# A gated recurrence dissolved into the end of the convolution and into the masked attention of a decoder kernel

## The chip, the cores and the metric

One core of a Trainium2 chip runs the whole program. The metric is the device time of one execution in microseconds. Before the change three runs took 3234.93, 3235.93 and 3240.06 us; their median, 3235.93 us, is the time before. About 0.2% (6.5 us) is what such a measurement can tell from no change.

## The reference, cut to what matters

The model is a decoder of four layers with three sublayers each, on x of 128 sequences x 64 tokens x 128 features, all in float32. Every sublayer ends as `x = layernorm(x + f(x))`. The change concerns three neighbours: the convolution with experts that ends layer 2 (`L2_ffn`), the gated recurrence that begins layer 3 (`L3_attn`), and the masked cross-attention after it (`L3_xattn`). The recurrence is

```python
xn = x / jnp.maximum(jnp.sqrt(jnp.sum(x * x, -1, keepdims=True)), 1e-12) * jnp.sqrt(128.) * gamma
q, kv, a = jnp.split(jnp.einsum('bnd,ed->bne', xn, W_qkva), 3, axis=-1)
# h[n] = sigmoid(a[n]) * h[n-1] + kv[n], along the 64 tokens of a sequence
out = q * h
```

The masked attention has 16 heads of 8 features over 64 keys, with a boolean mask of its own for each sequence, an output projection and a bias. The convolution sublayer has a router, eight small experts (SiLU), an RMS norm and a small GELU bottleneck.

## The kernel before, in words

The 8192 tokens are cut into 16 chunks (`NC`) of 512 tokens, that is 8 sequences; `X[c]` holds chunk c in SBUF, token on the partition, throughout. Sublayers follow one another as functions in a list `steps`; each loops over the chunks in a software pipeline that is written out by hand. Each engine takes its instructions in one order. This order follows the program text, except that a scheduler may move an instruction forward to fill a hole that it foresees; `tc.issue_after(i)` keeps what is inside behind instruction i if it runs on the same engine.

PSUM is used in two rings: `wide` tiles (pool psA, five banks) for scores and expert outputs, and `bank` tiles (pool psB, three banks) for everything else. A `bank` tile is the one that was given out three requests ago, so the matmul that fills it waits until that earlier tile has been read. SBUF work tiles come by tag from `SPACES` in the same way (most tags have two buffers, `r` has three).

**The convolution, `ffn_conv` (from L1620).** Eight turns of two chunks. A turn i computes eight groups of expert outputs (`units`, L1687: two matmuls of 512 columns and two bias matmuls on TensorE, two SiLU on ScalarE, one product of 1024 columns on VectorE, sums on VectorE and GpSimd) and takes in between the steps of two generators: `begin(i + 1)`, the convolution and routing of the next turn, and `end(i - 1)`, the end of the turn before. `end` has these steps: two transposes of the expert sums; two output projections `z`, with square and row sum; the RMS root together with the layernorm root of the turn before that (`norm`, L1757: one Newton chain on VectorE for both); then for each chunk the scaling of `acc` by the root and `normw` (L1735, four VectorE instructions of 128 columns), the transposes of `acc` on TensorE and the new residual on GpSimd; the down projection with GELU; the up projection and the residual sum (L1753). The main loop deals them out by `take` at the groups g of the next turn: two at g = 1, three at g = 3, two at g = 6, one at g = 7, the rest at g = 0 of the turn after. The end of the last turn runs alone after the loop (L1800).

**The recurrence, `attn_scan` (from L1808).** A stage of its own, 20 turns. A turn i does in this order: row sum of the squares of chunk i and layernorm statistics of chunk i - 4 (VectorE); the squares of chunk i + 1 (ScalarE, L1839); one Newton chain for both roots (`rsqrt`, L335, eleven small VectorE instructions); the scaling of chunk i by its root (two blocks on ScalarE, L1864, two on GpSimd, L1866); the normalised chunk i - 4 written back to X (ScalarE, L378); `recalled(i - 3)`, which transposes h back on TensorE and adds X (L1835); `project(i - 1)`: four transposes, the multiplication by gamma (ScalarE, L330), q, kv and gate as three matmuls of 512 columns (L1816, L1819), the sigmoid (ScalarE, L1821), a zero at every sequence start (GpSimd, L1823), the recurrence itself as one VectorE scan instruction over 512 columns (L1825) and its product with q (L1826).

**The masked attention, `xattn_masked` (from L1499), in the frame `mha` (from L1118).** The loop runs c from -2 to 16 and works on three chunks at once. TensorE's order in one iteration: second part of the weights of chunk c's first half, transposes of chunk c + 2 (`load`), `values(c - 1, 1)` (L1268), scores of the first half of chunk c + 1 (L1193) with their mask matmuls (L1529), transposes of the attention output of chunk c - 1, values of v (L1170), `weights(c, 1)` (L1231, mask L1535, maxima L1243), `values(c, 0)`, scores of the second half of chunk c + 1, projections q and k of chunk c + 2 (L945), the output projection (L1331), the first weights of chunk c + 1 up to the point where they need the maxima `mT` (L1218, copied by VectorE, L1220). VectorE reduces each group of scores to maxima (L1201), unpacks the masks (L1517), divides (L1273, L1282) and does the layernorm; ScalarE does the exponentials (L1250) and copies; four places `aside(c, k, ...)`, k = 0 to 3, let foreign work in. Before the change that is `kept` alone: the routing of the last sublayer, from c = 2 on one step at k = 2, from c = 11 on many.

Of the kernel before, what the change touches and what calls it, by code (L numbers as in the profile page):

```python
# [234 lines left out]
def tile_decoder(ctx: ExitStack, tc: tile.TileContext, a, out):  # L235
# [882 lines left out]
    def mha(prepare, wv, finish, mask=None, diff=False, aside=lambda c, k, seen: None):  # L1118
# [166 lines left out]
        on, late, spread = range(NC), (), None  # L1285
        for c in range(-2, NC + 1):
# [17 lines left out]
            if c in on:  # L1304
                weights(c, 1)
                behind = values(c, 0)
            aside(c, 2, (behind, spread))
# [191 lines left out]
    def xattn_masked():  # L1499
# [7 lines left out]

        def prepare(c, s):
            m = work("t1", (P, BPC * 2 * S // 4), "mu").bitcast(U8), VX[c % 2][:, used + 512 : used + 768].bitcast(U8)
            for x, src in zip(m, rows_of):  # L1510
                for g in range(4):
                    nc.sync.dma_start(out=x[32 * g : 32 * g + 32], in_=src[c])
            then = begin(c, s)

            def step(n):
                f = (work("ye", (P, 512), "mf") if n == 0 else VX[c % 2][:, used : used + 512]).bitcast(BF16)
                V.tensor_scalar(f, m[n], 0.0, NEG, ALU.is_equal, ALU.mult)  # L1517
                store[c, n] = f.rearrange("p (b n k) -> p b n k", b=BPC, n=2)
                return then(n)

            return step

        def mask(c, hf, s, t):
# [16 lines left out]
            mask=mask, aside=kept,  # L1540
# [79 lines left out]
    def ffn_conv():  # L1620
# [83 lines left out]
        def end(i):  # L1704
# [27 lines left out]
            for n in pair:  # L1732
                h = acc[n]
                for t in range(TPC):
                    V.scalar_tensor_tensor(h[:, t, :], h[:, t, :], y[:, 0, n, t : t + 1], row("normw"), ALU.mult, ALU.mult)  # L1735
                hT.append(transposed(h, "oT"))
                b = with_bias(2 * i + n, "upb")
                G.tensor_tensor(b, b, h, ALU.add)
                base.append(b)
                yield  # L1740
# [35 lines left out]
        for i in range(turns):  # L1776
            b = begin(i + 1) if i + 1 < turns else none
            e = end(i - 1) if i else none
            for g in range(8):
# [10 lines left out]
                elif g == 4:  # L1790
                    take(b, 2)
                elif g == 5:
                    take(b)
                elif g == 6:
                    take(e, 2)
                elif g == 7:
                    take(e)
            tail = e
        take(tail)
        for _ in end(turns - 1):  # L1800
            pass
# [6 lines left out]
    def attn_scan():  # L1808
        w = W[9]
        xs, hs, rs = {}, {}, {}  # L1810
        kept = work("h", (P, 8, 512), "scan")

        def project(c):
            xT = transposed(xs.pop(c), "xT", scale=col("gamma"))
            q = bank("q_ps")
            mm(q, w[:, 0, :], xT, start=True, stop=True)  # L1816
            ps = [wide("kva_ps") for _ in range(2)]
            for k in range(2):
                mm(ps[1 - k], w[:, 2 - k, :], xT, start=True, stop=True)  # L1819
            g = work("qT", name="gate")  # L1820
            A.activation(g, ps[1], AF.Sigmoid)  # L1821

            G.memset(g.rearrange("p (b s) -> p b s", b=BPC)[:, :, 0:1], 0.0)  # L1823
            h = hs[c] = kept[:, c % 8]
            V.tensor_tensor_scan(h, g, ps[0], 0.0, ALU.mult, ALU.add)  # L1825
            V.tensor_tensor(h, h, q, ALU.mult)  # L1826

        def recalled(c):
            h = hs.pop(c)
# [4 lines left out]
            r = rs[c] = work("r", (P, TPC, D))  # L1834
            V.tensor_tensor(r, y.rearrange("p (t d) -> p t d", t=TPC), X[c], ALU.add)  # L1835

        def squares(c):
            s = xs[c] = work("tmp", (P, TPC, D), "sq")
            A.activation(s, X[c], AF.Square)  # L1839


        squares(0)
        for i in range(NC + 4):
            v = sm.tile([P, 2, TPC], F32, tag="lnv2", name="lnv2")
            a_, b_ = i, i - 4
            if a_ < NC:
                V.tensor_reduce(v[:, 0], xs[a_], AX.X, ALU.add)
                V.tensor_scalar(v[:, 0], v[:, 0], 1e-24, None, ALU.max)
            else:
                G.memset(v[:, 0], 1.0)  # L1850
            if b_ >= 0:
                r = rs.pop(b_)
                mv = ln_stats(r, v[:, 1])
            else:
                G.memset(v[:, 1], 1.0)
            if a_ + 1 < NC:
                squares(a_ + 1)
            y = rsqrt(v.rearrange("p n t -> p (n t)"), 2 * TPC, "rms")
            if a_ < NC:
                V.tensor_scalar(y[:, :TPC], y[:, :TPC], math.sqrt(D), None, ALU.mult)  # L1860
                xn = xs[a_] = work("o", (P, TPC, D), "xn")
                for t in range(TPC):
                    if t % 2:
                        A.activation(xn[:, t, :], X[a_][:, t, :], AF.Identity, scale=y[:, t : t + 1])  # L1864
                    else:
                        G.tensor_scalar(xn[:, t, :], X[a_][:, t, :], y[:, t : t + 1], None, ALU.mult)  # L1866
            if b_ >= 0:
                ln_apply(b_, r, mv, y[:, TPC:], on_act=True)
            if 0 <= i - 3 < NC:
                recalled(i - 3)  # L1870
            if 0 <= i - 1 < NC:
                project(i - 1)
# [28 lines left out]
    def ffn_switch():  # L1901
# [8 lines left out]
        attn_alibi, xattn_padded, ffn_conv, attn_scan, xattn_masked, ffn_switch,  # L1910
# [25 lines left out]
```

## Time and profile before

| | us |
|---|---|
| median of three runs | 3235.93 |
| profiled execution | 3240.21 |
| its span | 3238.4 |
| recurrence alone on the engines, from 2542.0 to 2650.0 of the span | 108.0 |
| `mT` of chunk 0 and of chunk 11 copied (L1220) | 2673.74 and 2877.68 |

The profile comes from one hardware-traced execution. Times within it are microseconds from the start of the span. A row of a group names the line, the engine (PE is TensorE, PEld its weight loads, DVE VectorE, ACT ScalarE, POOL GpSimd, SP the queue that issues most DMAs), the operation, output <- input, shapes and count; then the busy time, the mean of one in ns, and the idle time of that engine just before with what ended it. A timeline row is start, duration, instruction, and in brackets the idle time before it. A row of a table of stretches gives for each engine the busy time and, in brackets, the number of instructions, then the granted TensorE clock (1 is full speed) and DMA. Matmul durations overlap: the pitch from one start to the next is what a matmul costs. The copies of `mT` mark the masked attention: one per iteration, the first at the end of iteration c = -1.

### The profile page before, as it was taken

The numbers are of one execution on the slowest core, as the hardware profiler recorded it, in microseconds if no ns is written. First come the engines' busy times: TensorE is split into PE (matmuls) and PEld (weight loads), VectorE is DVE, ScalarE is ACT, GpSimd is POOL, SyncE is SP. The second block draws the span as 40 slices with busy tenths as digits, with TensorE's granted clock in tenths as the row PEclk, the third lists the DMA queues.
The fourth block names the chain that finished last, engine by engine and source line by source line (L and its number), as shares of the span: only waits on it lengthen the run. The fifth ranks groups of instructions, "written<-read, shape, count | busy, mean of one in ns | idle before, by whom it ended". The sixth has DMA issues, their size and how long they took to land. (4 is left out here: it accounts for less than half of the span.)

```text
span 3238.4 us, 110324 instructions
## 1 busy us (share of the span) xinstructions
PE 2889.3 (89%) x47200; PEld 2120.7 (65%) x47200; DVE 1979.3 (61%) x7116; ACT 1638.5 (51%) x3130; POOL 1470.8 (45%) x1500
## 2 busy tenths in 40 slices
PE   5999899988887999999999989998888669997993
PEld 3789866656666777666677767763444337776893
DVE  3732289767776666332366656666778876675245
ACT  3444388745444555333356545643445546654453
POOL 4477554245554444211244445556666223336154
PEclk9999999999998999999999989988998789998997
DMA  5578711000003000000000000000000000001584
GB/s 143 153 210 261 224 52 34 8 2 3 3 3 93 4 4 4 4 1 1 14 4 4 4 5 4 4 12 1 1 1 7 4 1 19 18 13 59 182 263 143
DMA packets 142459, 159.23 MB, mean 49 GB/s; under 512 B 16720, under 2 KB 118096, under 8 KB 141968
## 3 DMA queue, kind: packets, MB, share of 16 engines
q1 hardware_dynamic: 128064, 123.65, 12.8%
q0 software_dynamic: 13184, 27.03, 3.3%
q8 instruction: 370, 6.06, 0.8%
q10 hardware_dynamic: 720, 1.50, 0.2%
q14 instruction: 121, 0.99, 0.1%
HBM read 121.44 MB, written 30.67 MB: 47 GB/s over the span
## 5 line engine op out<-in xcount | busy, mean ns | idle before, releaser
L1201 DVE TENSOR_REDUCE m<-s_ps 128x8 f32<-128x512 f32 x640 | 397.5, 684 | 146.3 <-PE s_ps L1529 50.5
L1250 ACT ACTIVATE e<-t_ps 128x512 f32<-128x512 f32 x640 | 329.9, 601 | 152.9 <-PE t_ps L1243 152.4
L1268 PE MATMUL av_ps<-vx,e 128*64 128x18 f32 (+1 forms) x10240 | 341.1, 216 | 7.3 <-issue 7.3
L1268 PEld LDWEIGHTS av_ps<-vx,e 128*64 128x64 f32 x10240 | 322.5, 140 | 28.1 <-issue 21.5
L1145 POOL TENSOR_SCALAR eb<-qT,small 128x512 f32<-128x512 f32 x80 | 131.5, 1643 | 432.6 <-ACT qT L948 197.6
L774 ACT ACTIVATE hT<-h_ps,aux 128x256 f32<-128x256 f32 x496 | 207.1, 470 | 219.6 <-PE h_ps L772 124.6
L1231 PE MATMUL t_ps<-eb,kT 32*64 32x128 f32 x10240 | 283.4, 287 | 6.6 <-ACT e L1250 2.2
L805 POOL DMA_INDIRECT got<-l_rout,pli x192 | 193.0, 1005 | 178.0 <-issue 64.4
L380 POOL TENSOR_SCALAR x<-xb,lnmv,ln_y 128x128 f32<-128x128 f32 x240 | 188.7, 798 | 173.6 <-DVE ln_y L345 173.6
L772 PE MATMUL h_ps<-ebT,rw 128*128 128x256 f32 x992 | 243.5, 390 | 14.4 <-DVE ebT L760 10.0
L1231 PEld LDWEIGHTS t_ps<-eb,kT 32*64 32x64 f32 x10240 | 200.2, 133 | 72.9 <-DVE m L1201 25.2
L785 PEld LDWEIGHTS yg<-rw,hT 128*128 128x128 f32 x1984 | 241.5, 192 | 6.4
L785 PE MATMUL yg<-rw,hT 128*128 128x128 f32 x1984 | 241.9, 275 | 0.0
L1193 PE MATMUL s_ps<-eb,qT 32*64 32x256 f32 x5120 | 217.4, 399 | 18.2 <-POOL eb L1145 9.6
L380 POOL TENSOR_SCALAR x<-r,lnmv,ln_y 128x128 f32<-128x128 f32 x100 | 79.4, 807 | 293.3 <-DVE ln_y L345 246.9
L786 DVE TENSOR_TENSOR yo<-yg,aux 128x256 f32<-128x256 f32 x124 | 52.5, 424 | 260.8 <-PE yg L785 260.7
L1273 DVE RECIPROCAL rc<-av_ps 128x32 f32<-128x32 f32 (+1 forms) x192 | 61.7, 322 | 244.5 <-PE av_ps L1268 244.1
L772 PEld LDWEIGHTS h_ps<-ebT,rw 128*128 128x128 f32 x992 | 184.1, 196 | 38.3 <-DVE ebT L760 12.6
L747 POOL DMA_INDIRECT aux<-in_x_dram,plt x156 | 158.3, 1015 | 60.4 <-issue 26.1
L1143 ACT ACTIVATE eb<-qT,small 128x512 f32<-128x512 f32 x160 | 106.8, 715 | 128.9 <-POOL qT L1370 123.6
L1145 POOL TENSOR_SCALAR eb<-kT,small 128x512 f32<-128x512 f32 x80 | 145.3, 1816 | 21.8 <-ACT kT L950 10.9
L1193 PEld LDWEIGHTS s_ps<-eb,qT 32*64 32x64 f32 x5120 | 114.4, 134 | 57.1 <-POOL eb L1145 13.4
(437 smaller groups left out, 6446.1 us busy)
## 6 DMA issues: line engine op xcount, KB each, us to landing
rw<-in_l0w_dram SPq DMA_DIRECT2D x78, 512.0 KB
rw<-in_l3w_dram SPq DMA_DIRECT2D x46, 512.0 KB
l_rout<-yo SPq DMA_DIRECT2D x124, 128.0 KB
aux<-xd SPq DMA_DIRECT2D x46, 128.0 KB
aux<-in_l0b_dram SPq DMA_DIRECT2D x78, 66.0 KB
xd<-vx SPq DMA_DIRECT2D x5, 1024.0 KB
x<-in_x_dram SPq DMA_DIRECT2D x16, 256.0 KB
cin<-in_ctx_dram SPq DMA_DIRECT2D x16, 256.0 KB
```

Source lines behind the costliest of these rows:

```text
L380: (V if on_dve else G).tensor_scalar(X[c][:, t, :], r[:, t, :], mv[:, t, 0:1], y[:, t : t + 1], ALU.subtract, ALU.mult)
L747: s.gather = G.indirect_dma_start(out=eb[:, i, :], out_offset=None, in_=x[:, :], in_offset=bass.IndirectOffsetOnAxis(ap=tokens[:, 2 * g + ...
L772: s.pe = mm(ps[:, j * GR : (j + 1) * GR], w1[:, (k + j) * P : (k + j + 1) * P], ebT, start=True, stop=True)
L774: s.act_ins = A.activation(hT[k + j], ps[:, j * GR : (j + 1) * GR], s.act, bias=v[:, k + j : k + j + 1])
L785: s.pe = mm(y[:, i * P : (i + 1) * P], hT[k][:, i * P : (i + 1) * P], w2[:, k, :], start=(k == 0), stop=(k == FK - 1))
L805: s.gather = G.indirect_dma_start(out=got[i][k][:, t, :], out_offset=None, in_=s.rout[b][:, :], in_offset=bass.IndirectOffsetOnAxis(ap=whe ...
L1145: ins = (G if h == 2 else V).tensor_scalar(dst, x, mine, None, ALU.mult)
L1193: mm(ps[g][j * S : (j + 1) * S, u * 256 : (u + 1) * 256].rearrange("p (h k) -> p h k", h=4), rows32(s["q"], g)[:, b], rows32(s["eb"], g)[: ...
L1201: last = V.tensor_reduce(s["m"][:, g, 2 * hf : 2 * hf + 2, :].rearrange("p t h -> p (t h)"), ps[g].rearrange("p (n k) -> p n k", k=S), AX. ...
L1231: mm(ps[g][i * S : (i + 1) * S].rearrange("p (a u j q) -> p a u j q", u=2, a=2, j=2)[:, :, u, j, :], rows32(s["k"], g)[:, b], rows32(s["eb ...
L1250: last = A.activation(e[:, g, :], ps[g], AF.Exp, scale=scale)
L1268: mm(av[j * S : (j + 1) * S, 8 * (u - u0) + n, :], ev[:, n // 2, n % 2, u, j, :], vx[:, 2 * (2 * hf + u) + j, n, :], start=True, stop=True,)
```

## The change

The function `attn_scan` and its place in `steps` go. A class `Scan` has five steps for a chunk, and a call runs those that have not been run: `root` (squares, row sum, layernorm statistics of chunk c - 2, one Newton chain for both), `scale` (the scaling by the root, and chunk c - 2 normalised into X), `turn` (transposes, gamma), `run` (three matmuls, sigmoid, scan, product) and `sum` (h transposed and added to X in place). The layernorm of a chunk thus comes with the root of the chunk after next. The zero at the sequence starts moves from GpSimd to VectorE; kv, gate and q come from the ring of three banks, with gate the first to be multiplied.

In the convolution's last turn and in its last end the steps of chunks 0, 1 and 2 are dealt out. In the masked attention `recurrent` takes the place of `kept`, calls it, and then deals out a chunk's five steps over a turn and a half: root at k = 1, scale at k = 2, turn at k = 3 of iteration c for chunk c + 5, then run at k = 0 and sum at k = 2 of the next iteration. Thirteen chunks (3 to 15) go there. The tags of their work tiles (`o`, `xT`, `oT`, `r`) are those of the attention's own tiles.

In `end` of the convolution the scaling of `acc` (L1735) becomes a step of its own, for both chunks at once, and the loop takes it at g = 4 in place of g = 6; this holds for every turn.

```diff
-                weights(c, 1)
+                last_e = weights(c, 1)
                 behind = values(c, 0)
-            aside(c, 2, (behind, spread))
+            aside(c, 2, (behind, last_e, spread))
...
-            mask=mask, aside=kept,
+            mask=mask, aside=recurrent,
...
                     V.scalar_tensor_tensor(h[:, t, :], h[:, t, :], y[:, 0, n, t : t + 1], row("normw"), ALU.mult, ALU.mult)
+            yield
+            for n in pair:
+                h = acc[n]
                 hT.append(transposed(h, "oT"))
...
                 elif g == 4:
+                    take(e)
                     take(b, 2)
...
+                if i == turns - 1:
+                    scan(((0, "root"), (0, "scale"), (), (0, "turn"), (0, "run"), (), (0, "sum", 1, "root"), (1, "scale"))[g])
...
-        for _ in end(turns - 1):
-            pass
+        last = (1, "turn"), (1, "run"), (), (1, "sum"), (2, "root"), (2, "scale"), (), (2, "turn"), (2, "run"), (2, "sum")
+        for n, _ in enumerate(end(turns - 1)):
+            scan(last[n])
...
+        def root(s, c):
+            v = sm.tile([P, 2, TPC], F32, tag="lnv2", name="lnv2")
+            mv, x = None, None
+            if c < NC:
+                x = work(s.tags["x"], (P, TPC, D), "sq")
+                A.activation(x, X[c], AF.Square)
+            if c >= 2:
+                mv = ln_stats(X[c - 2], v[:, 1])
...
+        def run(s, c):
+            w, xT = W[9], s.at[c]
+            kv, ps, q = (bank(n) for n in ("kv_ps", "gate_ps", "q_ps"))
+            for n, d in (2, ps), (1, kv), (0, q):
+                mm(d, w[:, n, :], xT, start=True, stop=True)
+            g = work(s.tags["gate"], name="gate")
+            A.activation(g, ps, AF.Sigmoid)
+
+            V.memset(g.rearrange("p (b s) -> p b s", b=BPC)[:, :, 0:1], 0.0)
+            h = s.at[c] = work(s.tags["h"], name="scan")
+            V.tensor_tensor_scan(h, g, kv, 0.0, ALU.mult, ALU.add)
             V.tensor_tensor(h, h, q, ALU.mult)
...
+    def recurrent(c, k, seen):
+
+        kept(c, k, seen)
+        with ExitStack() as behind:
+            for i in seen:
+                if i:
+                    behind.enter_context(tc.issue_after(i))
+            scan(((c + 4, "run"), (c + 5, "root"), (c + 4, "sum", c + 5, "scale"), (c + 5, "turn"))[k])
...
-        attn_alibi, xattn_padded, ffn_conv, attn_scan, xattn_masked, ffn_switch,
+        attn_alibi, xattn_padded, ffn_conv, None, xattn_masked, ffn_switch,
```

More of the change, by code (lines that the diff above doesn't have):

```diff
@@ L1284, in mha @@
         nlam = lam_neg() if diff else None
-        on, late, spread = range(NC), (), None
+        on, late, spread, last_e = range(NC), (), None, None
         for c in range(-2, NC + 1):
@@ L1506, in xattn_masked @@
         used = BPC * 8 * 18
+        scan.tags.update({"x": "o", "xT": "xT", "gate": "oT", "h": "r"})
         def prepare(c, s):
+            assert c in scan.whole
             m = work("t1", (P, BPC * 2 * S // 4), "mu").bitcast(U8), VX[c % 2][:, used + 512 : used + 768].bitcast(U8)
@@ L1805, in ffn_conv, with __init__, __call__, scale @@
         return S_[turns - 1]["silu"].ins
[L1808 to L1825, printed above, removed]
+    class Scan:
+        tags = {"x": "tmp", "xT": "kT", "gate": "qT", "h": "tmp"}
+        def __init__(s):
+            s.at, s.whole, s.begun = {}, set(), set()
+        def __call__(s, steps):
+            for c, name in zip(steps[::2], steps[1::2]):
+                if (c, name) not in s.begun and c < (NC + 2 if name in ("root", "scale") else NC):
+                    s.begun.add((c, name))
+                    getattr(s, name)(c)
+        def root(s, c):
[6 more added lines that the diff above has]
+                mv = ln_stats(X[c - 2], v[:, 1])
+            else:
+                G.memset(v[:, 1], 1.0)
+            if c < NC:
+                V.tensor_reduce(v[:, 0], x, AX.X, ALU.add)
+                V.tensor_scalar(v[:, 0], v[:, 0], 1e-24, None, ALU.max)
+            else:
+                G.memset(v[:, 0], 1.0)
+            y = rsqrt(v.rearrange("p n t -> p (n t)"), 2 * TPC, "rms")
+            if c < NC:
+                V.tensor_scalar(y[:, :TPC], y[:, :TPC], math.sqrt(D), None, ALU.mult)
+            s.at[c] = x, y, mv
+        def scale(s, c):
+            x, y, mv = s.at[c]
+            if c < NC:
+                for t in range(TPC):
+                    if t % 2:
+                        A.activation(x[:, t, :], X[c][:, t, :], AF.Identity, scale=y[:, t : t + 1])
+                    else:
+                        G.tensor_scalar(x[:, t, :], X[c][:, t, :], y[:, t : t + 1], None, ALU.mult)
+            if c >= 2:
+                ln_apply(c - 2, X[c - 2], mv, y[:, TPC:], on_act=True)
+                s.whole.add(c - 2)
+        def turn(s, c):
+            x = s.at[c][0]
+            ps = bank("xT_ps")
+            for t in range(TPC):
+                nc.tensor.transpose(ps[:, t * P : (t + 1) * P], x[:, t, :], ident)
+            xT = s.at[c] = work(s.tags["xT"], name="xT")
+            A.activation(xT, ps, AF.Identity, scale=col("gamma"))
+        def run(s, c):
[8 more added lines that the diff above has]
+            V.tensor_tensor_scan(h, g, kv, 0.0, ALU.mult, ALU.add)
@@ L1826, in project, with sum @@
             V.tensor_tensor(h, h, q, ALU.mult)
-        def recalled(c):
-            h = hs.pop(c)
+        def sum(s, c):
+            h = s.at.pop(c)
             y = bank("y")
@@ L1833, in recalled @@
                 nc.tensor.transpose(y[:, q], h[:, q], ident)
[L1834 to L1872, printed above, removed]
+            added(c, y, X[c])
+    scan = Scan()
+    def recurrent(c, k, seen):
[5 more added lines that the diff above has]
+            scan(((c + 4, "run"), (c + 5, "root"), (c + 4, "sum", c + 5, "scale"), (c + 5, "turn"))[k])
     n_rows = [(len(cs) * CT + E8 * (GR - 1)) // GR * GR for cs in SWITCH_BATCHES]
```

## The prediction

> **What bounds the kernel now.** I read the page's slices first, then the busy times by stretch, the waits of each engine within a stretch, the groups of the recurrence stage, and two iterations of the masked attention instruction by instruction. The table of stretches carries the argument:
>
> ```profile
> core 0: us, PE busy (x) PEld busy (x) DVE busy (x) ACT busy (x) POOL busy (x), PEclk, DMA share, GB/s
> 2493.50:2529.00 35.50, 18.95 (x83) 11.02 (x82) 31.00 (x92) 15.34 (x29) 16.22 (x18) 0.71 0.04 12
> 2529.00:2673.70 144.70, 94.05 (x457) 49.98 (x463) 118.16 (x514) 77.61 (x173) 34.88 (x62) 0.83 0.01 3
> 2542.00:2650.00 108.00, 70.11 (x230) 36.41 (x228) 95.46 (x429) 57.78 (x132) 18.77 (x48) 0.90 0.00 1
> 2673.70:2877.70 204.00, 195.79 (x5494) 148.67 (x5483) 132.60 (x399) 125.13 (x216) 77.42 (x68) 1.00 0.07 18
> 2877.70:2901.20 23.50, 21.21 (x516) 14.67 (x497) 15.47 (x49) 13.36 (x24) 8.55 (x8) 1.00 0.05 14
> 2901.20:2921.10 19.90, 17.86 (x513) 13.86 (x515) 18.28 (x69) 10.37 (x19) 8.11 (x8) 1.00 0.01 4
> ```
>
> The first two rows run from the row sums of the convolution's next-to-last end (L1727) to the first `mT` of the masked attention: 180.2 us, in which VectorE is busy 149.2 and TensorE idles a third, at a lowered clock. The third row is the recurrence alone: bound by VectorE (95.5 of 108). The fourth is eleven iterations of the masked attention, 18.55 us each: bound by TensorE (96%) at full clock, VectorE busy 12.1 us of each. The change thus moves work from a stage that VectorE bounds into one that TensorE bounds. The price in the second depends on what TensorE adds and on whether VectorE keeps up.
>
> **What goes and what stays before the attention.** In the changed program's order the same stretch, from the same L1727 to the first `mT`, holds 69 us of VectorE work at the durations of before (30 up to the last turn's L1727, 39 after it). I walked both parts along their chains. First part: zero, scan and product of chunk 0 (2.5 us) and the Newton steps of two roots lie ahead of the scaling of `acc`, which begins at 13 us (13.1 before, when three of the last groups of experts stood ahead of it). Then the last group, sums, transposes, z: 34 us, against 35.5. Second part: root of chunk 2 at 9.7, its gate on TensorE at 13 to 17, a GELU and a sigmoid table between, scan and product to 19.6, the residual sums and two layernorms to 28; chunk 0 of the attention is projected meanwhile; root of chunk 3 to 32, its transposes, scores of chunk 0 to 35, reductions, run of chunk 3, root of chunk 4, second half's reductions, `mT`: 50.5 us. Together 84.5 against 180.2: **-95.7 us**. Such walks leave out small waits; +15 is the likely bound, -6 the other, were chunk 3 not to hold up the first scores.
>
> **What TensorE gains in an iteration.** Pitches at full clock, from the timeline of one iteration:
>
> ```profile
> 2757.61 1.13 PE L945 MATMUL qT_ps<-xT,w_l3x 128*128 128x512 f32 x2
> 2758.57 1.02 PE L945 MATMUL kT_ps<-ctx,w_l3x 128*128 128x512 f32 x2
> 2759.43 1.05 PE L1331 MATMUL y<-w_l3x,oT 128*128 128x128 f32 x8
> ...
> 2748.54 0.66 PE L325 MATMUL oT_ps<-ident,o 128*128 128x128 f32 x4
> 2749.13 1.15 PE L1170 MATMUL v_ps<-w_l3x,ctx 128*64 128x64 f32 x32
> ```
>
> From start to start a product of 512 columns costs 0.86 to 0.96 us, four transposes 0.59. A chunk of the recurrence is three and eight: 2.7 + 1.2 = **3.9 us**, with nothing idle to hide it in.
>
> **What VectorE gains.** These are its groups in the stage of before:
>
> ```profile
> L1825 DVE TENSOR_TENSOR_SCAN scan<-gate,kva_ps 128x512 f32<-128x512 f32 x11 | 13.4, 1216 | 4.7 <-PE kva_ps L1819 2.2 <-POOL xn L1866 1.3 <-POOL gate L1823 1.2
> L366 DVE BATCH_NORM_STATS2 lnst<-r 128x6 f32<-128x128 f32 x40 | 8.7, 280 | 0.0
> L1826 DVE TENSOR_TENSOR scan<-scan,q_ps 128x512 f32<-128x512 f32 x11 | 7.5, 678 | 0.0
> L1847 DVE TENSOR_REDUCE lnv<-sq 128x4 f32<-128x512 f32 x9 | 6.1, 677 | 0.0
> L343 DVE TENSOR_TENSOR rms_u<-rms_y 128x8 f32<-128x8 f32 x28 | 4.7, 167 | 1.0
> ```
>
> By pitch: scan 1.18, product 0.63, row sum 0.65, residual sum 0.65, statistics 0.84 + 0.36, fifteen small ones at 0.2, the moved zero 0.12: **7.4 us** a chunk. The attention's own VectorE instructions come to 13.7 by pitch, so 21.1 in all. VectorE waits 6.0 us an iteration now (29.5 for scores at L1201, 24.5 for `av` at L1273, 11.9 at L1517, over the eleven); 7.4 us fit only as far as they fall into these waits.
>
> **ScalarE and its tables.** An iteration gains sigmoid 0.6, square 0.63, two scalings 0.8, xT 0.67, four normalisations 1.9, and two table switches, since sigmoid and exponential alternate where before one load served the whole stage:
>
> ```profile
> 2673.33 1.33 ACT L1143 ACTIVATE eb<-kT,small 128x512 f32<-128x512 f32 x2
> 2674.68 1.28 ACT L1250 ACT_TABLE_LOAD   x1
> 2675.98 2.06 ACT L1250 ACTIVATE e<-t_ps 128x512 f32<-128x512 f32 x4
> ```
>
> The load starts 0.02 us after the last instruction and the exponential 0.02 after the load: 1.3 us a switch. The Trainium skill (ScalarE: Activation LUTs, *What ACT_TABLE_LOAD costs*) says a switch costs about 2.66 us, a drain of 1.38 with it[...]: this speaks against the change. By the row ScalarE has 19 us of work in an iteration; by the page 21.8, the sigmoid and what hangs on it 1.4 us later and the second half's chain 0.8, some 26 us more over 12 iterations. I go by the row.
>
> **The walk through an iteration** (0 is the copy of `mT`). TensorE's transposes for chunk c + 5 put the rest off by 0.6. ScalarE: xT and square, exponentials 2.3 to 4.35, xT copy to 5.0, table to 6.3. The gate takes the bank of that xT by rotation, so it starts at 5.05, not 4.4; kv and q end at 7.7, the scores at 9.2 (5.3 before). The sigmoid is done at 6.9; VectorE, idle since 5.25, does zero, scan and product to 8.9, four reductions to 11.5, statistics and Newton chain to 16.1, mask and `av` to 17.6. The transposes of h need that `av`'s bank: TensorE waits from 16.8 to 17.6. Second scores end at 19.7 (14.4 before), reductions at 21.8, then eb, `hl`, residual sum, as before: `mT` at 23.8, against 18.7. VectorE is then at 21.1 of 23.8: almost the bound. Per iteration **+5.1**: 3.9 is TensorE's own, 1.2 new waits. Bounds: +3.9 if another bank comes free earlier; +6.6 if GpSimd's sum of two tensors (L393) holds VectorE up beside it. Before, small VectorE operations took 1.2 us in place of 0.17 beside such sums in the convolution.
>
> Iterations 0 to 10: 11 x 5.1 = +56. Iteration 11 (23.5 us, already full of routing) gets run, sum and a layernorm: between +3.3 and +7, I take +5. Iteration 12 has VectorE at 18.3 of 19.9 and gets a layernorm of 4.2: +3. Together **+64 us**.
>
> **The edit in the convolution.** TensorE waits for `acc` before its transposes (20.2 us in six turns). The eight scalings now stand together in VectorE's order, in front of the routing's small steps instead of among them, so the last is done 1.5 to 2 us sooner; but TensorE still waits for the first, and two bias matmuls that slipped in between stand later. 0.5 us a turn, six turns: **-3**, bounds -8 and +3; the routing's end is no later, as VectorE's total is the same. GpSimd loses its memset, worth nothing, since it idles half of each iteration. The mask and weight loads keep their queue order; the weights of the attention now have 30 us in place of 100 to arrive, which hides a load of 256 KB.
>
> **The sum**, on the profiled execution's 3240.2 (span 3238.4 and 1.8 around it): -95.7 + 64 - 3 = -34.7, 3205.5. The median of the runs lies 4.3 below that execution: **3201 us**.
>
> **Rivals.** *TensorE alone* (20%): VectorE's additions fall wholly into its waits, +3.9 an iteration: 11 x 1.2 and about 2 less, 3186 us. For it: 6.0 us of waits; against: they lie at three places, one after the new wait for the sigmoid. *The front does not shrink* (18%): in the end of the convolution each chunk's five steps are a chain over four engines, with two or three table loads per chunk, and the attention's first scores stand behind chunk 3; 20 us more there, 3221. For it: TensorE's clock of 0.71 in that stretch. *Slower* (10%): VectorE becomes the attention's bound in series. Its order is fixed, so if none of the 7.4 us falls into the old waits (they recur after each TensorE result) and the wait for the sigmoid, 1.7, comes on top, an iteration grows by 9.1: 4.0 more than forecast, in 12 iterations 48 us, 3249. It decides from +8 an iteration (35 us over 12 is 2.9 above 5.1). Likeliest case (52%): 3201, alone 3188 to 3216. That the recurrence isn't dissolved as said can be excluded: its steps stand in the changed program's order.
>
> From these cases: faster by over 0.2% 0.87, within 0.05, slower 0.08. The range, 3180 to 3234, reaches from below TensorE alone with a short front up to the edge of no change.
>
> **What would show it.** The first `mT` about 96 us sooner after the same L1727; `mT` every 23 to 24 us, with VectorE over 85% busy and 24 switches of about 1.3 us; TensorE waiting at the gate for xT's copy and at the h transposes for L1282. It is wrong if the period exceeds 26, if VectorE still waits 6 us an iteration, or if the front takes over 100 us.

## The result, and the profile after

The changed kernel takes 3232.06 us (median of 20 runs, 3221.47 to 3241.02), the kernel before, in runs shared with it, 3237.80 us (20 runs, 3228.12 to 3248.34): a ratio of 0.9978, 95% interval 0.9969 to 0.9988. It is faster by 5.7 us, where 35 were forecast. The profiled execution of after took 3228.74 us, its span is 3226.9; the one of before 3240.21 and 3238.4. So the two traces differ by 11.5 us, of which 5.7 are the medians' difference; the profiled execution of after lies 3.3 below its median and that of before 2.4 above the shared one.

The same stretches as in the prediction's first table, for the kernel after. The mark of before's line L1727, the end of the convolution's row sums, is the one that stands at L1730 in after. The rows run from the next-to-last mark to the last one; from there to the first `mT`; iterations 0 to 10 of the masked attention; iteration 11; iteration 12:

```profile
core 0: us, PE busy (x) PEld busy (x) DVE busy (x) ACT busy (x) POOL busy (x), PEclk, DMA share, GB/s
2496.40:2533.60 37.20, 28.01 (x107) 14.64 (x105) 31.51 (x88) 19.12 (x33) 16.06 (x17) 0.72 0.03 11
2533.60:2592.40 58.80, 41.62 (x239) 17.30 (x240) 36.61 (x145) 30.65 (x61) 13.36 (x13) 0.67 0.02 5
2592.40:2856.90 264.50, 254.91 (x5632) 174.06 (x5631) 204.20 (x707) 194.53 (x336) 96.13 (x91) 0.98 0.05 14
2856.90:2887.10 30.20, 27.66 (x533) 17.76 (x532) 21.37 (x75) 17.92 (x31) 11.22 (x11) 0.94 0.04 11
2887.10:2909.80 22.70, 19.14 (x513) 14.13 (x519) 21.39 (x91) 12.76 (x24) 9.12 (x9) 0.98 0.01 3
```

The front shrank from 180.2 to 96.0 us, and the eleven iterations grew from 203.9 to 264.5: TensorE still bounds them (254.9 of 264.5 busy), VectorE has gone from 65% to 77%. Put side by side over the whole span, stretch by stretch:

| stretch | before | after | difference | forecast |
|---|---|---|---|---|
| start to the mark ahead of the five long turns | 2240.6 | 2238.3 | -2.3 | 0 |
| five long turns of the convolution | 217.8 | 223.2 | +5.4 | -3 with the sixth |
| its sixth turn | 35.0 | 34.9 | -0.1 | |
| front: last turn and the way to the first `mT` | 180.2 | 96.0 | -84.2 | -95.7 |
| iterations 0 to 10 | 203.9 | 264.5 | +60.6 | +56 |
| iteration 11 | 23.6 | 30.2 | +6.6 | +5 |
| iteration 12 | 19.9 | 22.7 | +2.8 | +3 |
| the rest | 317.2 | 317.1 | -0.1 | 0 |

The differences sum to -11.3 (-11.5 by the spans, the rest is rounding), the forecasts to -34.7.

The growth of the iterations is not the same all along. Iterations 3 to 10 took 152.9 us before and 194.0 after, 19.1 and 24.2 each: +5.1, as forecast. Iterations 0 to 2 took 51.0 and 70.5: +6.5 each, and 4.2 of the 4.6 us over the forecast lie there. Their granted clock was 0.94, 0.86 and 1.00 in after and 1.00 before.

**One iteration of after**, on TensorE, with only the lines of the recurrence and of the first scores; the columns are start, time, engine and line. The period runs here from `mT` at 2711.55 to 2735.69:

```profile
2711.29 0.63 PE L1869 MATMUL xT_ps<-ident,sq 128*128 128x128 f32 x4
2715.98 1.12 PE L1877 MATMUL gate_ps<-xT,w_l3a 128*128 128x512 f32 x2
2717.04 0.64 PE L1193 MATMUL s_ps<-eb,qT 32*64 32x256 f32 x2
2717.61 1.13 PE L1877 MATMUL kv_ps<-xT,w_l3a 128*128 128x512 f32 x2
2718.57 1.02 PE L1877 MATMUL q_ps<-xT,w_l3a 128*128 128x512 f32 x2
2719.52 0.90 PE L1193 MATMUL s_ps<-eb,qT 32*64 32x256 f32 x23
...
2728.35 1.07 PE L1193 MATMUL s_ps<-eb,qT 32*64 32x256 f32 x6
2729.44 0.63 PE L1891 MATMUL y<-ident,scan 128*128 128x128 f32 x4
```

The gate starts 4.43 after `mT` (the walk had 5.05, after a wait for xT's copy that does not come), the transposes of h at 17.9 (17.6), the next `mT` stands at 24.14 (23.8). Two things cost TensorE more than the products: a pair of score matmuls stands alone between gate and kv and takes 0.57 from start to start, and the transposes of h follow a stop of about 1.1 us, since their bank is that of `av` (L1282 on VectorE ends at about 2729.3). The walk had the second and missed the first.

VectorE's waits in the eleven iterations of after (in all, times, longest):

```profile
DVE gate L1881 <- ACT gate L1879: 18.2, 11, 7.2
DVE m L1201 <- PE s_ps L1532: 10.0, 19, 1.4
DVE rc L1273 <- PE av_ps L1268: 7.6, 10, 5.4
DVE scan L1883 <- PE kv_ps L1877: 7.0, 10, 0.9
DVE x L399 <- PE y L1891: 6.9, 8, 1.1
```

They sum to some 50 us, 4.5 an iteration, where they were 6.0 before; VectorE's 77% is less than the 85% that the prediction named as a sign. The old waits for scores and `av` (29.5 and 24.5) became small and new ones, for the sigmoid above all, took their place. VectorE does not bound the iterations, so the rival on the slow side didn't happen.

**The way to the first `mT`.** TensorE in after, from the first scores to the products of chunk 3 (the bracket is idle time before and its releaser). Then the granted clock, third number from the end, in steps of 3.41 us; in this trace every change of the clock falls on an edge of such a step:

```profile
2563.86 1.56 PE L1193 MATMUL s_ps<-eb,qT 32*64 32x256 f32 x24 [2.97 <-POOL eb L1145]
2568.06 0.47 PE L1869 MATMUL xT_ps<-ident,sq 128*128 128x128 f32 x1 [2.65 <-POOL sq L1860]
...
2576.05 2.08 PE L1877 MATMUL gate_ps<-xT,w_l3a 128*128 128x512 f32 x2
2577.91 1.92 PE L1877 MATMUL kv_ps<-xT,w_l3a 128*128 128x512 f32 x2
2579.62 1.91 PE L1877 MATMUL q_ps<-xT,w_l3a 128*128 128x512 f32 x2
```

```profile
2560.94:2564.35 3.41, 0.49 (x18) 0.39 (x21) 2.55 (x14) 2.35 (x5) 2.57 (x2) 1.00 0.00 0
2564.35:2567.76 3.41, 1.07 (x16) 0.24 (x4) 2.51 (x18) 3.41 (x10) 0.35 (x1) 0.50 0.00 0
2567.76:2571.18 3.42, 3.12 (x16) 1.15 (x16) 0.00 (x0) 1.79 (x5) 0.83 (x2) 0.50 0.00 0
2571.18:2574.59 3.41, 3.41 (x13) 0.99 (x12) 0.00 (x0) 0.69 (x1) 0.00 (x0) 0.50 0.00 0
2574.59:2578.00 3.41, 3.41 (x12) 1.40 (x12) 1.89 (x3) 1.11 (x2) 0.00 (x0) 0.50 0.00 0
2578.00:2581.42 3.42, 3.42 (x5) 0.93 (x3) 2.08 (x4) 0.60 (x1) 0.00 (x0) 0.50 0.00 0
2581.42:2584.83 3.41, 3.41 (x77) 2.48 (x82) 3.11 (x13) 1.19 (x2) 0.00 (x0) 1.00 0.03 5
```

The clock falls at 2564.35, behind the wait of 2.97 us for GpSimd's `eb` and ahead of chunk 3: it is not chunk 3 that brings it down. Chunk 3's first transpose then stands inside the row of first scores and waits 2.65 us for GpSimd's scaling (L1860). The scores behind it wait too, and the clock stays at half until 2581.42, so that each product takes 1.7 to 1.9 us instead of 0.95. VectorE meanwhile stands still, and gets its first reduction 42 us after the last L1730, where the walk had the scores done at 35. The root of chunk 3 ends at 33.6 (32 in the walk), so most of the loss comes behind it:

```profile
2552.75 0.07 DVE L1881 MEMSET gate<- 128x8 f32 x1 [8.62 <-ACT gate L1879]
2575.67 1.89 DVE L1201 TENSOR_REDUCE m<-s_ps 128x8 f32<-128x512 f32 x3 [8.37 <-PE s_ps L1532]
```

### The profile page after: what moved, and what is told of

Same layout as the page of the kernel before. It is cut to its first block, busy times and chain, and to the rows that moved or that the text cites. A ratio compares the mean times of both kernels' runs of the same rounds, so it can differ in the third digit from the quotient of the medians.

```text
span 3226.9 us, 110276 instructions
## 1 busy us (share of the span) xinstructions
PE 2915.1 (90%) x47200; PEld 2121.9 (66%) x47200; DVE 1987.5 (62%) x7110; ACT 1673.5 (52%) x3158; POOL 1471.7 (46%) x1480
## 5 line engine op out<-in xcount | busy, mean ns | idle before, releaser
L1193 PE MATMUL s_ps<-eb,qT 32*64 32x256 f32 x5120 | 230.6, 401 | 15.4 <-POOL eb L1145 13.4
L1193 PEld LDWEIGHTS s_ps<-eb,qT 32*64 32x64 f32 x5120 | 116.9, 134 | 74.2 <-issue 17.9
```

Of the source, the lines that this page charges most:

```text
L1193: mm(ps[g][j * S : (j + 1) * S, u * 256 : (u + 1) * 256].rearrange("p (h k) -> p h k", h=4), rows32(s["q"], g)[:, b], rows32(s["eb"], g)[: ...
```

## The experiments

The theory at the start was that the mechanism is as forecast, and that small steps were missed: chunk 3 in front of the first scores, and in an iteration the bank of `av` and the scattered scores. Its rivals: ScalarE's table switches in the iteration, the clock alone in the front, and chance in the convolution's turns. Ratios are to runs of the kernel before that were taken together with the run. In the last five runs, from `g1_both_repairs` on, every kernel takes some 190 to 210 us more (before: 3426 and 3446 us), so only ratios and stretches are compared there.

**The convolution's edit alone, and the change without it.** `c1_scaling_only` is before with two places of the diff:

```
+            yield
+            for n in pair:
+                h = acc[n]
                 hT.append(transposed(h, "oT"))
...
                 elif g == 4:
+                    take(e)
                     take(b, 2)
```

> The kernel before with the convolution's edit alone: the scaling of acc as a step of its own, taken at g = 4. In the profile of the whole change the five stretches from L1727 to L1727 of the convolution's middle turns took 223.2 us against 217.9 before. Theory A (this edit lengthens each turn, since five transposes that wait for five scalings now stand ahead of the two bias matmuls that two expert groups wait for): the same stretches again about 1 us longer each, so the kernel 5 to 8 us slower than before, ratio 1.0015 to 1.0025. Theory B (the recorded step: it gains 0.5 us a turn, and the 5 us are scatter between executions): 3 us faster or nothing to be told from none, ratio 0.999 to 1.000, stretches 215 to 218 us.

Measured: 3247.57 us (12 runs) to 3242.99 (23), ratio 1.001, 0.9995 to 1.0025. `c2_without_scaling` is after with these lines taken back.

> The whole change without the convolution's edit: the scaling again in the step of the transposes, taken at g = 6; the recurrence is dealt out as in the change. Theory A (the edit costs 5 to 8 us): faster than the change by that, ratio to before 0.995 to 0.9965. Theory B (the edit is worth nothing or gains 3 us): ratio to before 0.998 to 0.999, as the change itself (0.9978).

Measured: 3233.27 us (12 runs), ratio 0.9963, 0.9947 to 0.9979; front 93.9 us, iterations 0 to 10 261.8. The edit is not told from zero by the times, and what the change gains is in its other parts. The five long turns were 219.5 us in the first and 221.5 in the second, between 218 and 223. How much of that is scatter is taken up at the end of this section.

**No table switches.** `m1_no_switch`: the gate's Sigmoid becomes a Tanh, which shares the exponential's table, for chunks from 3 on. It leaves the right gate out.

```
-            A.activation(g, ps, AF.Sigmoid)
+            A.activation(g, ps, AF.Tanh if c > 2 else AF.Sigmoid)
```

> The change with a tanh in place of the sigmoid for chunks 3 to 15, which needs no other table than the exponential's: it leaves the right gate out of the computation, the instructions and their data flow are the same, and 24 table loads go from the masked attention. Theory A (a switch costs 1.3 us of a ScalarE that has slack): the period of the copies of mT falls from 24.0 to between 23.3 and 24.0 us, since only the gate's 1.3 us lie ahead of the scan. Theory B (the switches are what holds the iteration up, by the drain that the skill states or by what queues behind them): the period falls by 2 us or more, to 22 us or less.

Measured: one run of 3240.45; the steady period is 24.1 as in after, iterations 0 to 10 262.9 instead of 264.5. ScalarE in one iteration, first of after, then of this kernel:

```profile
2716.08 1.28 ACT L1879 ACT_TABLE_LOAD   x1
2717.37 0.60 ACT L1879 ACTIVATE gate<-gate_ps 128x512 f32<-128x512 f32 x1
2724.01 1.28 ACT L1250 ACT_TABLE_LOAD   x1
2725.30 2.06 ACT L1250 ACTIVATE e<-t_ps 128x512 f32<-128x512 f32 x4
```

```profile
2746.49 0.60 ACT L1879 ACTIVATE gate<-gate_ps 128x512 f32<-128x512 f32 x1 [1.09 <-PE gate_ps L1877]
2754.26 2.06 ACT L1250 ACTIVATE e<-t_ps 128x512 f32<-128x512 f32 x4 [0.94 <-PE t_ps L1243]
```

Where the load stood, ScalarE now idles 1.09 and 0.94 us for TensorE. A load of 1.28 that fills a wait of 1.09 or 0.94 costs ScalarE 0.2 to 0.3 us, and the period nothing. The Trainium skill's price of 2.66 us a switch (ScalarE: Activation LUTs, *What ACT_TABLE_LOAD costs*), which I had not taken, would by its estimate have added 26 us; the trace has the instruction behind each load 0.01 us after its end.

**The sum a stretch sooner.** In after, chunk c + 4's transposes of h come behind the first half's `av`, whose bank they take. `m3_sum_earlier`:

```
-            scan(((c + 4, "run"), (c + 5, "root"), (c + 4, "sum", c + 5, "scale"), (c + 5, "turn"))[k])
+            scan(((c + 4, "run"), (c + 4, "sum", c + 5, "root"), (c + 5, "scale"), (c + 5, "turn"))[k])
```

> The change with sum (the transposes of h and X's residual sum) one place earlier, at k = 1 in place of k = 2. In the change these transposes stand behind the second scores' first six matmuls and wait for the PSUM bank of av, which VectorE reads only after a Newton chain: 1.1 us of TensorE an iteration by the pitches. Theory A (that wait is a real part of the new period): the transposes fill in behind v's matmuls without a wait, and the period of mT falls from 24.1 to 23.0 to 23.3 us. Theory B (VectorE, with 21 us of its own instructions in a row, sets the period): the wait moves elsewhere, 23.8 to 24.1 us.

Measured: one run of 3224.16 beside 3238.51; the period falls to 23.0, iterations 0 to 10 to 257.8. Theory A: the wait for `av`'s bank cost 1.1 us an iteration in the steady period. The first three iterations did not gain (71.7 us for 70.5).

**And the scores kept behind the three products.** `m5_sum_and_whole_run` adds to this that `run` keeps its last product's instruction, `recurrent` returns it, and the scores are issued behind it:

```
-            aside(c, 0, (behind, spread))
-            seen = scores(c + 1, 0) if c + 1 in on else None
+            front = aside(c, 0, (behind, spread))
+            with tc.issue_after(front) if front else nullcontext():
+                seen = scores(c + 1, 0) if c + 1 in on else None
...
```

> As before (sum at k = 1), and the first scores are kept behind the last of the chunk's three products on TensorE, so that no lone 32-row score matmul stands between gate and kv. In the profile of the change that lone one costs 0.57 us from start to start, where in a row 16 of them take 0.9 us. Theory A (both are the price of how the steps are laid in, on a TensorE that bounds the iteration): period 22.5 to 22.8 us, and 8 to 15 us less in time than the change, ratio to before 0.993 to 0.996. Theory B (VectorE sets the period): 23.5 us or more, ratio about 0.998. In the front chunk 3's run now stands ahead of all the first scores; that may cost or gain some us there.

Measured: 3213.88 us (4 runs) to 3238.51 (7), ratio 0.9926, 0.9908 to 0.9944: Theory A. Its TensorE rows:

```profile
2703.81 1.12 PE L1878 MATMUL gate_ps<-xT,w_l3a 128*128 128x512 f32 x2
2704.89 1.10 PE L1878 MATMUL kv_ps<-xT,w_l3a 128*128 128x512 f32 x2
2705.82 1.02 PE L1878 MATMUL q_ps<-xT,w_l3a 128*128 128x512 f32 x2
2706.77 1.12 PE L1193 MATMUL s_ps<-eb,qT 32*64 32x256 f32 x32
2709.92 0.66 PE L1892 MATMUL y<-ident,scan 128*128 128x128 f32 x4
```

The three products are one run, the scores another of 32 in a row, and the transposes of h come 6 us after the gate instead of 13. Most periods are 22.5. Over iterations 3 to 10 the mean is 19.1 us before, 24.2 in after, 23.3 with the sum sooner and 22.7 here. So of the 5.1 us that after pays in each, 1.0 is the bank, 0.5 the scattered scores, and 3.6 is left for TensorE's own work, costed at 3.9. Iterations 0 to 2 take 71.1 us here, no less than in after; what they pay beyond the others stays open.

The front is shorter too: from the last L1730 to the first `mT` 54.6 us, for 58.9 in after and 58.9 with the sum sooner alone. The scores are held behind chunk 3's three products in the front as well, so chunk 3 stands whole in front of them.

**The front.** `f1_chunk3_later` moves chunk 3's steps behind the first scores:

```
+            if c == -2:
+                scan(((), (3, "root"), (3, "scale"), ())[k])
+            elif c == -1:
+                scan(((), (3, "turn", 4, "root"), (3, "run", 4, "scale"), (3, "sum", 4, "turn"))[k])
...
```

> The change with chunk 3's turn, run and sum later by one place or more in the first two iterations (turn at k = 1 of iteration -1, run at k = 2, sum at k = 3), so that its transposes no longer stand among the first scores. In the change TensorE waits 2.65 us there for GpSimd's scaling, falls to a granted clock of 0.50 for 10 us, and VectorE idles 8.4 us for the scores. Theory A (this wait and the clock after it are what the walk missed): front from the last L1730 to the first mT 50 to 54 us in place of 58.9. Theory B (the five steps' chain sets it): chunk 3's steps come later and delay chunk 1's X, first iterations longer by as much: front shorter, but mT of chunk 2 no earlier, 105 us after the last L1730 as before.

Measured: one run of 3225.4; from the last L1730 to the first `mT` 53.5 us instead of 58.9, iterations 0 to 10 262.7, no longer than in after. Theory A: 5.4 us of the front are chunk 3's stand in the scores. The wait of 2.97 us and the fall of the clock are there as in after; the clock stays at half for 10.2 us in place of 17.1.

`f2_warm` puts four more products of 512 columns, which nothing reads, behind chunk 0's projections, to keep TensorE's clock up into the first scores.

> The change with four more matmuls of 512 columns behind the projections of the masked attention's chunk 0, whose results nobody reads; they fill TensorE's wait before the first scores (2.97 us in the profile of the change). Theory A (the second part of the front took 58.8 us in place of 50.5 because TensorE, after its idle stretches, ran at about half the granted clock: a product of 512 columns 1.9 us in place of 0.96): the matmuls after them run at full pitch, the first reductions L1201 come 3 to 6 us sooner, and the stretch from the last L1730 to the first mT shrinks to 53 to 56 us. Theory B (the chain through VectorE, ScalarE and GpSimd sets this stretch, TensorE's clock is only a sign of its idling): the added work hides or delays, 58 to 62 us.

Measured: one run of 3244.23; the stretch takes 58.2 us, but the first iteration 28.0 in place of 23.0, and iterations 0 to 10 take 267.4. The rows show why it tells little:

```profile
2568.12 1.88 PE L1163 MATMUL idle_ps<-qT,w_l3a 128*128 128x512 f32 x4
2569.84 1.88 PE L1163 MATMUL idle_ps<-kT,w_l3a 128*128 128x512 f32 x4
2575.61 0.47 PE L1873 MATMUL xT_ps<-ident,sq 128*128 128x128 f32 x1 [2.88 <-POOL sq L1864]
```

```profile
2571.41:2574.82 3.41, 1.32 (x23) 0.53 (x22) 2.93 (x21) 3.03 (x8) 0.00 (x0) 1.00 0.00 0
2574.82:2578.24 3.42, 2.62 (x16) 1.12 (x16) 0.03 (x1) 2.48 (x8) 1.18 (x2) 0.50 0.00 0
```

The clock was up for the first scores, and fell to 0.50 within the wait of 2.88 us for chunk 3: here the wait comes first and the clock follows. `f3_later_and_warm` has both edits.

> The same with four more matmuls of 512 columns behind the first projections, which nobody reads. With those alone (f2_warm) TensorE was back at a clock of 0.98 at the first scores, and fell to 0.50 again after the 2.9 us wait for chunk 3. Theory A (the clock is a cause): without the second wait the clock stays above 0.9 through the first scores and the front is 1 to 3 us shorter than with the later steps alone. Theory B (the clock is only a sign): equal to it within 1 us, or longer.

Measured: one run of 3226.3, the stretch 55.8 us against 53.5 without the extra products. They cost more than the clock returns. No run takes the clock's own share of the front apart from the waits'.

**Both repairs, and each kernel a second time.** `g1_both_repairs` has the edits of `m5_sum_and_whole_run` and `f1_chunk3_later`.

> Both repairs at once: chunk 3's transposes, products and sum later in the first two iterations, and in the iterations the sum a stretch sooner with the scores' matmuls kept behind the three products. Theory A (front and iterations each pay for a step that stands in front of the scores, and the two are independent): the second part of the front about 53 us, the periods about 22.5, so about 5 us off the kernel with the sum and the whole run, near 3209 us where before is at 3238, a ratio near 0.991. Theory B (what the front gives up comes back in the first iterations, since chunk 3's steps only move there): no faster than the sum and the whole run alone, ratio 0.9926, with the first two periods above 24.

Measured: 3401.03 us (6 runs) to 3426.21 (11), ratio 0.993, 0.9907 to 0.9953; the stretch 53.5, iterations 0 to 10 254.7, the second of them 27.7. Theory B: nothing over the one repair. In `m5_sum_and_whole_run` the stretch was already 54.6, and the 1.1 us gained on it are lost again in iterations 0 to 2 (73.0 us for 71.1). Keeping chunk 3 whole in front of the scores and moving it whole behind them are worth about the same.

> The changed kernel as it is, profiled a second time, to see which stretches repeat. Theory A (the front and the periods are set by the order of the work, the convolution scatters): front 96 and second part 59 within 2 us, iterations 0 to 10 264 within 2, the five turns of the convolution anywhere from 217 to 224. Theory B (the front with its low clock scatters as well): second part off by over 3 us.

> The kernel before as it is, profiled a second time. Theory A: front 180 and iterations 0 to 10 204, each within 2 us, and the five turns of the convolution anywhere from 217 to 224. Theory B (the edit of the scaling made the turns longer): the turns stay at 218 in the kernel before and at 223 in the changed one.

Measured, after: front 95.9, its second part 58.9, iterations 0 to 10 264.7, all as in the first profile. Before: front 180.2, but iterations 0 to 10 209.1, beyond what Theory A allowed: eight periods agree within 0.5 us with the first profile, and three are 1.6 to 1.8 longer, at a granted clock of 0.92 where it had been 1.00. By this pair the iterations grew by 55.6, by the first by 60.6, so a forecast of +56 is not told from either.

The five turns of the convolution are 223.3 and 216.9, near the first profiles (223.2 and 217.8). That looks like Theory B, and as if the turns did not scatter. The other traces say otherwise. Seven more kernels start the same instructions in the same order in these turns, on TensorE, VectorE, ScalarE and GpSimd alike. The second column is the time from the first mark to the next edge of the clock's steps of 3.41 us:

| trace | edge, us | the five turns, us | sum |
|---|---|---|---|
| `m1_no_switch` | 0.47 | 44.5, 43.9, 45.3, 43.7, 43.6 | 221.1 |
| after | 1.78 | 45.0, 45.3, 44.0, 45.3, 43.6 | 223.2 |
| `r1_after_again` | 1.87 | 45.0, 45.2, 44.0, 45.4, 43.7 | 223.3 |
| `g1_both_repairs` | 1.97 | 45.1, 45.2, 44.0, 45.3, 43.7 | 223.3 |
| `m5_sum_and_whole_run` | 2.13 | 45.2, 43.9, 44.3, 44.3, 44.3 | 221.9 |
| `f3_later_and_warm` | 2.35 | 46.9, 44.4, 43.7, 43.8, 45.3 | 224.2 |
| `f1_chunk3_later` | 2.69 | 46.9, 44.4, 43.7, 45.3, 43.7 | 224.0 |
| `m3_sum_earlier` | 3.18 | 44.3, 44.4, 43.7, 43.8, 45.3 | 221.6 |
| `f2_warm` | 3.19 | 44.3, 44.4, 43.8, 43.7, 45.3 | 221.5 |

The same work takes from 221.1 to 224.2 us, and the turns agree where the edges lie alike (after, r1 and g1; m3 and f2). So the two profiles of after agreed by the chance of their edges. What holds is the difference between the orders: 216.9, 217.5 and 217.8 us in the three traces with the order of before, 3.2 to 7.3 less than in these nine.

**What makes the turns longer.** The trace of after shows chunk 0's root in the second of them. It is written in the last turn, and the scheduler had moved it there:

```profile
2313.34 0.65 DVE L1844 TENSOR_REDUCE lnv<-sq 128x4 f32<-128x512 f32 x1
...
2316.45 0.17 DVE L1850 TENSOR_SCALAR rms_y<-rms_y 128x4 f32<-128x4 f32 x1
```

`t1_root_held` keeps it behind the last turn's first experts:

```
+                    with tc.issue_after(S_[i]["silu"].ins) if g == 0 else nullcontext():
                         scan(((0, "root"), (0, "scale"), (), (0, "turn"), (0, "run"), (), (0, "sum", 1, "root"), (1, "scale"))[g])
```

> The changed kernel with chunk 0's root kept behind the first experts of the convolution's last turn; in the changed kernel its square, row sum and Newton chain had been placed in the second of the five long turns. Theory A (those 14 VectorE instructions, about 3.4 us, are what makes the second turn 45.3 instead of 42.0, since VectorE is hardly idle there): the second turn back at 42 to 42.5, the five turns about 220 instead of 223.2, and at most 3 us more where the root now stands. Theory B (the turns differ by the clock alone): the second turn stays above 44.

Measured: one run of 3448.63 beside 3445.61; the turns are 46.8, 44.1, 44.0, 43.7 and 45.3, together 223.9. Theory A falls as it stood: the second turn is 1.2 shorter, not 3, and the first has become 1.8 longer. `t2_all_undone_and_repaired` holds the root, takes the scaling's edit back and has both repairs.

> All at once: the scaling's edit taken back, chunk 0's root kept behind the first experts of the last turn, chunk 3's steps later in the first two iterations, the sum a stretch sooner and the scores kept behind the three products. Theory A (the convolution's five turns lose 5.4 us to the root and to the edit, the front 5.4 to chunk 3, the iterations 1.2 each to the wait for a bank and to the scattered scores): five turns near 218, front second part 53.5, iterations 0 to 10 about 254, together 20 to 24 us under the changed kernel, a ratio to before near 0.990. Theory B (what the turns lose is the clock's, whatever stands in them): five turns stay above 221 and the ratio near 0.993, as with the two repairs alone.

Measured: 3420.63 us (6 runs) to 3445.61 (11), ratio 0.9927, 0.9906 to 0.9947. The turns are 42.6, 42.5, 44.0, 44.1 and 44.3, together 217.5 as in before. The turns speak for Theory A, the ratio for neither. The fourth and fifth turn, first of before, then of after (the third number from the end is the clock):

```profile
2370.10:2414.20 44.10, 39.77 (x154) 19.47 (x152) 33.49 (x79) 20.55 (x38) 27.34 (x28) 0.88 0.00 1
2414.20:2458.50 44.30, 39.82 (x154) 19.35 (x152) 33.11 (x79) 20.55 (x38) 27.57 (x26) 0.88 0.00 1
```

```profile
2372.50:2417.80 45.30, 39.68 (x154) 19.95 (x152) 34.90 (x78) 20.43 (x38) 27.63 (x28) 0.85 0.00 1
2417.80:2461.50 43.70, 39.56 (x154) 19.39 (x152) 34.55 (x79) 20.43 (x38) 27.39 (x26) 0.89 0.00 1
```

VectorE is busy 1.4 us longer in each of them with the edit, where the prediction had taken its total as unchanged. It is tempting to read 43.7 us at a clock of 0.89 against 44.1 to 44.3 at 0.88 as the half microsecond that was costed. But `m5_sum_and_whole_run`, with the edit, takes 44.3 us three times at 0.88, so the gain isn't shown.

What the traces show is this. Chunk 0's root, without the edit (`c2_without_scaling`), makes the second turn 45.2 instead of 42.0 us, and the five 221.5; held back, it makes the sixth 36.7 to 37.1 instead of 35.0. The edit without the root has two traces with one and the same order in the five turns: 219.5 in `c1_scaling_only` and 223.9 in `t1_root_held`. So with the root or with the edit the five turns come out longer than before, with the edit by 1.6 to 7.0 us, and its size can't be told closer from single traces. With the edit, 13 of 55 turns stand at a clock of 0.83 to 0.85 and take 45.3 us or more; without it none of 20 is under 0.88. Why the edit brings turns to the lower clock stays open.

## Why the prediction was wrong in size

The direction was right, and so was the mechanism of the two large terms: a shorter front, paid for on TensorE in the iterations. 3232.06 lies inside the range, close to its upper edge, which stood for no change. The gain of 35 us was the difference of -98.7 and +64. In the traces 23.4 us of it are missing: 11.5 in the front, 8.3 in the convolution's turns, 4.6 in iterations 0 to 10 and 1.6 in iteration 11, less 2.6 elsewhere. The first is a term that was mis-sized, the second a step that failed.

- **The front, -95.7 forecast, -84.2 measured.** The term that was mis-sized most. The last turn took 37.2 for 34, the way to the first `mT` 58.9 for 50.5. I had said that chunk 3's transposes come before the scores, at the time its root is ready; in fact they stand within the scores and hold them 2.65 us, at a clock that was already down to half and stays there. Three products take 5.4 instead of 2.8 us, and VectorE gets no reduction for 8.4. Moving chunk 3 away gave 5.4 us back, so this is shown. Of the other 3, 1.6 were lost by the end of chunk 3's root, and no run takes them apart, nor the 3.2 of the last turn (36.9 to 37.2 us in seven traces with its order). The bound of +15 that I gave held it (+11.5), but the walk took TensorE at full clock, where the table of before shows 0.71 and 0.83 for these stretches; it was 0.72 and 0.67 after.
- **The iterations, +5.1 forecast, +5.1 measured** in iterations 3 to 10, and +6.5 in 0 to 2 (+60.6 in all, for +56; +55.6 in the second pair of profiles). Luck has a part in the 5.1: a lone pair of scores between gate and kv costs 0.5, which I had counted at its cost in a row, and the wait at the gate that I had did not come; the wait for `av`'s bank is 1.0 where I had 1.2 of new waits, and TensorE's own work comes to 3.6 where I had 3.9. The first three iterations I had priced like the others.
- **Iteration 11, +5 forecast, +6.6 measured**, within the bounds given; iteration 12 as forecast (+2.8 for +3).
- **The convolution, -3 forecast, +5.4 measured** in the traces. Here the step itself failed, and lay outside my bound of +3. I had put no price on where chunk 0's root would come to stand: it is in the second turn, which is 45.2 us with it and 42.0 without. And I had costed the edit at 0.5 us a turn gained, with VectorE's total the same; VectorE is busy 1.4 us longer in the turns shown, the gain isn't shown by any run, and with the edit alone the five turns came out 1.6 to 7.0 us longer. With the edit taken back and the root held, the turns are back at 217.5, so the two together are the cause; how the loss divides between root, edit and clock stays open.
- **The rivals.** *TensorE alone* was near to what the steady iteration could be: with two edits of order it costs 3.6 us more than before. The kernel then takes 0.9926 of before, still far from that rival's 3186 us. *The front doesn't shrink* named the right place, and the loss there is half of what it priced. *Slower* needed VectorE as the bound in series; it waits 4.5 us of 24 in an iteration.
- **Table switches.** By the row rather than the rule was right, and even the row's 1.28 us doesn't reach the period.

The medians put the gain at 5.7 where the traces show 11.5; single executions of one kernel differ by up to 20 us, so a profile of one can't settle 6 us. The front and most periods repeat within 0.5 us in a second profile and show where the time went; the turns repeat to about 3 us only.

## What to carry to other kernels

When the forecast is the difference of a large saving and a large cost, give each its own error and widen by both: a tenth of 96 and a tenth of 64 were most of the gain here. When work is moved between stages, look on every engine's order for where each piece comes to stand, since a piece that is written late can land in an earlier stage that nobody priced. On an engine that executes in order, put a long product run in one piece, ahead of the next group or behind it, and its later consumer behind no bank that another chain still holds: with both the change is 24.6 us faster than before, without them 5.7. When two profiles of one kernel agree, that does not yet show that a stretch repeats: other kernels that hold the same stretch in the same order are further samples of it.

## What the runs showed of the hardware

- TensorE's granted clock changed only at the edges of steps of 3.41 us. A step in which TensorE was busy 0.49 us (2560.94 of after) or 1.32 (2571.41 of `f2_warm`) was followed by a step at 0.50. It then stayed at 0.50 through steps with 3.12 and 3.41 us of transposes, score and mask matmuls, and came back at 2581.42, behind the first step filled with products of 512 columns. The Trainium skill (TensorE: Matmul & The Clock Gate, *Part 1: The HAM clock gate*) speaks of an idle window of about 3.4 us to lose the clock and about as much of sustained work to regain it, in windows that run free of the kernel. The length and the free running agree with the traces; the window here did not have to be wholly idle, and the measurement decides. Which matmuls count as work no run takes apart.
- The same order of instructions took 221.1 to 224.2 us over five turns in nine executions, and turn by turn the same where the edges of these steps lay alike (the table above).
- Two 32-row score matmuls alone between products of full height take 0.57 us from start to start, where a row of 32 takes 1.12 together.
- A switch of ScalarE's table took 1.28 us with 0.01 behind it, and nothing of the period where ScalarE would have waited for TensorE anyway.
- The whole kernel took 3427.67 us in `r1_after_again` and 3228.74 in the first profile, while its front, periods and turns agree.
